# Routed experts in an attention stream: up products with the experts' weights stationary, activations kept by inner unit

## The chip, the cores and the metric

The kernel runs on one core of a Trainium2 chip. The metric is the time of one execution in microseconds, lower being better. Times are compared as medians over runs on the same chip; the reading of the engines comes from one profiled execution.

## The reference

Two transformer layers run over 32 sequences of 256 tokens of width 128, all in float32. Each layer is adaptively normalised attention with 16 heads of 8, followed by 16 routed experts of inner width 64, of which each token takes two. Layer 1 has a shared expert of width 256 besides. Cut to the routed experts, which are what the change touches:

```python
# layer 0
gu = jnp.einsum('th,ehf->tef', x, gate_up_proj) + gate_up_proj_bias
gate, up = gu[..., ::2], gu[..., 1::2]
gate = jnp.minimum(gate, LIMIT)
up = jnp.clip(up, -LIMIT, LIMIT)                       # LIMIT = 7
act = (up + 1.0) * gate * jax.nn.sigmoid(gate * ALPHA) # ALPHA = 1.702
out = jnp.einsum('tei,eih,te->th', act, down_proj, scores)
out = out + jnp.einsum('te,eh->th', scores, down_proj_bias)
# layer 1, for each expert
h = jax.nn.silu(x @ wg) * (x @ wu)
acc = acc + cw[:, None] * (h @ wd)
```

`scores` and `cw` are zero except for the two chosen experts, so only those two have to be computed.

## The kernel before

**The stream.** The attention of both layers is cut into 32 chunks of 512 tokens, and each chunk into 16 steps, 512 steps in all. In every step TensorE (PE) computes scores twice (line 1767, `s`): once for the maxima of the unit 12 steps ahead, which VectorE (DVE) reduces at line 1150 (`mpad`), and once for the exponentials, which ScalarE (ACT) takes at line 1174 (`ex`). Eight products with the values follow (line 1186, `pv`). The banks that hold the scores for the maxima are two while experts run, and three otherwise. PE's scores of the next step therefore wait for DVE's reductions of this one. All other work of the layer (projections, transposes, norms, routing) hangs on one of the 16 places of a chunk, by tables of functions. The program order of every engine is written by this one loop over steps: nothing reorders it later.

**The experts.** Tokens are sent to DRAM rows sorted by expert (`hs`), one 128-token tile for one expert. A group is 8 chunks (the last has 6) and fills 80 tiles (64), in batches of four. Groups 0 and 1 are of layer 0, groups 2 and 3 of layer 1. Groups 0 to 2 run inside the stream, one batch in three steps, 60 batches in all; group 3 runs behind the stream, one batch a step, and is called quick. For a batch that begins at step s0, the loop plans in the stream:

- `load_bias` at s0-1 (layer 0 only): four DMAs, each sending one expert's 128 biases from the DRAM table `bgt` to all 128 partitions (`bg`, line 1325); `load` at s0-5: four DMAs of token rows (`hl`, line 1315).
- `turn` at s0: four transposes of the tokens (line 1358), copied by ACT (`keep_turned`, line 1364).
- `up` at s0+1: four products, tokens stationary, the expert's gate and up weights (128 columns) moving, read from `weights` at an offset in a PE register (line 1371, `gu`). The result has tokens on partitions.
- `act_1` at s0+2, `act_1b` at the end of s0+2 (layer 0, tanh on ACT) and `act_2` at s0+4: the activation, on DVE, lines 1388 to 1408. In layer 1 `act_1` does all of it.
- `turn_act` at s0+4: four transposes back to inner units on partitions (line 1414, `aT`), copied by ACT at s0+5 (`keep_act`, line 1418).
- `down` at s0+5 (line 1425, `y`), `weigh` at s0+6 on DVE (line 1436, `yw`), `put` at s0+6 (line 1443), the DMA back to DRAM.

The functions of a step are queued in three lists. `early` comes ahead of the step's reductions on DVE, `behind_` after them, and `late` is PE's work at the end of the step. Small products for routing and the shared expert (`jobs`) run at the end of steps divisible by three; batches begin at steps that leave a remainder of one, so a job falls on s0+2 when there is one. The reductions of a step stand on DVE behind everything in `early`. SyncE (SP) issues nearly all DMAs in program order, eight completion semaphores in turn, so that a DMA waits for the one eight before it.

Of the kernel before, what the change touches and what calls it, by code (L numbers as in the profile page):

```python
# [19 lines left out]
E, FI, FS = 16, 64, 256  # L20
EPS = 1e-5
P = 128
# [3 lines left out]
NT = CT // P  # L26
# [14 lines left out]
NPAIR = E // 2  # L41
ALPHA, LIMIT = 1.702, 7.0
# [34 lines left out]
V_BQ, V_BK, V_SQ, V_SK, V_KONE, V_QONE, V_BO, V_BG, V_BU, V_SG = 0, 2, 4, 6, 8, 9, 10, 11, 19, 27  # L77
# [4 lines left out]
def two_layers(  # L82
# [50 lines left out]
    dram = ctx.enter_context(tc.tile_pool(name="dram", bufs=1, space=bass.MemoryType.DRAM))  # L133
# [1 line left out]
    hs = [dram.tile([g.rows, HR], F32, tag=f"hs{g.k}", name=f"hs{g.k}") for g in groups]  # L135
    ys = [dram.tile([P * g.tiles, D], F32, tag=f"ys{g.k}", name=f"ys{g.k}") for g in groups]
    rows = [dram.tile([B, 7 * D], F32, tag=f"rows{l}", name=f"rows{l}") for l in range(2)]
    bgt = dram.tile([E, 2, FI], F32, tag="bgt", name="bgt")
    ctx.enter_context(
        tc.manual_schedule(engines={et.PE, et.Activation, et.DVE, et.Pool, et.SP})  # L140
    )
# [32 lines left out]
    vec = loaded("vec", vecs, [P, NVEC], nc.scalar)  # L174
# [165 lines left out]
    def constants_3():  # L340

        nc.gpsimd.iota(part, [[0, 1]], base=0, channel_multiplier=1, allow_small_or_imprecise_dtypes=True)
        nc.gpsimd.memset(ones, 1.0)
        nc.gpsimd.iota(iota_e, [[0, NT], [1, E]], base=0, channel_multiplier=0, allow_small_or_imprecise_dtypes=True)
        nc.gpsimd.memset(empty, 0.0)
        nc.gpsimd.iota(tile0, [[P, TILES]], base=0, channel_multiplier=0, allow_small_or_imprecise_dtypes=True)
        nc.gpsimd.memset(aT[FI : FI + 1], 2.0)
        nc.vector.tensor_scalar(below, pos[:, :P], part, None, ALU.is_gt)
        for s_, t in ebase.items():
            nc.vector.tensor_scalar(t, iota_e, float(s_), None, ALU.mult)  # L350
        nc.vector.tensor_scalar(upto, pos[:E, :E], part[:E], None, ALU.is_ge)
        nc.vector.tensor_copy(wr1g[:, E : E + 1], vec[:, V_SG : V_SG + 1])
        for g in groups:
            nc.sync.dma_start(hs[g.k][E * g.stride :, :], empty)
# [137 lines left out]
    def expert_biases():  # L492


        def pe(p):
            nc.tensor.transpose(p[: 2 * NPAIR, :P], vec[:, V_BG : V_BG + 2 * NPAIR], ident)

        def others(p):
            b_ = once.tile([P, NT, FI], F32, tag="s", name="bts")[: 2 * NPAIR]
            b_ = b_.rearrange("p q n -> p (q n)")[:, :P]  # L500
            nc.scalar.copy(b_, p[: 2 * NPAIR, :P])
            for n in range(2):
                for a_ in range(2):
                    nc.sync.dma_start(
                        bgt.rearrange("(q a) n i -> a n q i", a=2)[a_, n],
                        b_[n * NPAIR : (n + 1) * NPAIR, a_ * FI : (a_ + 1) * FI],
                    )

        return ("bt", pe, others)
# [724 lines left out]
    def table_jobs(g):  # L1234
# [71 lines left out]
            (f"look{k}", look_up, looked_up),  # L1306
        ]

    hl, es, bgs, xTs, gus, acs, yps, yws, pst, mids = {}, {}, {}, {}, {}, {}, {}, {}, {}, {}

    def load(g, b):
# [4 lines left out]
            if b == 0 and q == 0:  # L1316
                behind(ins, scattered[k])

    def load_bias(g, b):
        k = g.k  # L1320
        if g.l == 0:
            bgs[k, b] = once.tile([P, NT, 2 * FI], F32, tag="bg", name=f"bg{k}_{b}")
            flat = bgt.rearrange("e n i -> (e n i)").rearrange("(o f) -> o f", o=1)
            for q, v in enumerate(held(tables[k][:, 0, b * NT : (b + 1) * NT], et.SP, (E - 1) * P)):
                nc.sync.dma_start(
                    bgs[k, b][:, q, :], flat[:, bass.ds(v, P)].to_broadcast([P, P])
                )

# [4 lines left out]
    def bank_of(g, b, usual, n, name):  # L1333
        if begins_at[g.k, b] < NU - 1:
            return bank(usual, name)
        if n == 2 and b % 2 == 0:
            return bank("b", name)
        return end_bank(3 if n == 1 and b % 2 else n, name)
# [27 lines left out]
    def up(g, b):  # L1366
        k = g.k
        p = bank_of(g, b, "a", 2, f"gu{k}_{b}")
        gus[k, b] = p.rearrange("p (q n) -> p q n", q=NT)
        for q in range(NT):  # L1370
            nc.tensor.matmul(  # L1371
                gus[k, b][:, q, :],
                xTs[k, b][:, q, :],
                weights[g.l][0][:, bass.ds(es[k, b][q], P)],
                start=True,
                stop=True,
            )

    def act_1(g, b):
        k = g.k  # L1380
        gate, upv = gus[k, b][:, :, :FI], gus[k, b][:, :, FI:]
        s = once.tile([P, NT, FI], F32, tag="s", name=f"s{k}_{b}")
        a_ = once.tile([P, NT, FI], F32, tag="a", name=f"a{k}_{b}")
        acs[k, b] = a_
        if g.l == 0:
            g1 = once.tile([P, NT, FI], F32, tag="g1", name=f"g1{k}_{b}")
            bg = bgs[k, b]
            nc.vector.tensor_tensor(g1, gate, bg[:, :, :FI], ALU.add)
            nc.vector.tensor_tensor(a_, upv, bg[:, :, FI:], ALU.add)
            nc.vector.tensor_scalar(g1, g1, LIMIT, None, ALU.min)  # L1390
            nc.vector.tensor_scalar(a_, a_, LIMIT, -LIMIT, ALU.min, ALU.max)
            mids[k, b] = s, g1
        else:
            nc.scalar.activation(s, gate, AF.Tanh, scale=0.5)
            nc.vector.scalar_tensor_tensor(a_, s, 1.0, gate, ALU.add, ALU.mult)
            nc.vector.tensor_tensor(a_, upv, a_, ALU.mult)

    def act_1b(g, b):
        if g.l == 0:
            s, g1 = mids[g.k, b]  # L1400
            nc.scalar.activation(s, g1, AF.Tanh, scale=ALPHA / 2)

    def act_2(g, b):
        if g.l == 0:
            k = g.k
            s, g1 = mids[k, b]
            nc.vector.scalar_tensor_tensor(g1, s, 1.0, g1, ALU.add, ALU.mult)
            nc.vector.scalar_tensor_tensor(acs[k, b], acs[k, b], 1.0, g1, ALU.add, ALU.mult)

    def turn_act(g, b):  # L1410
        k = g.k
# [182 lines left out]
    for g in groups:  # L1594

        base = max(16 * (g.end + 1) + 11, free_from)
        if g is groups[-1]:

            base = max(base, NU - 1)
        else:  # L1600
            base += (1 - base) % 3
        starts[g.k] = base

        quick = g is groups[-1]
        products, rest = {}, {}
        for b in range(g.batches):
            s0 = base + b * (1 if quick else 3)
            begins_at[g.k, b] = s0
            back, end_ = (2, 4) if quick else (4, 6)

            plan(s0 - (1 if b else 2), early, load_bias, g, b)
            plan(s0 - ((3 if quick else 5) if b else 2), early, load, g, b)
            plan(s0 + 2, behind_, act_1b, g, b)
            plan(s0 + end_, behind_, put, g, b)
            for f, at in ((turn, 0), (up, 1), (down, back + 1), (turn_act, back)):
                products.setdefault(s0 + at, {})[f] = b
            for f, at in ((weigh, end_), (keep_act, back + 1), (act_2, back), (act_1, 2), (keep_turned, 1)):
                if quick:
                    rest.setdefault(s0 + at, {})[f] = b
                else:  # L1620
                    plan(s0 + at, early, f, g, b)
        for at, what in rest.items():

            for f in (keep_turned, act_1, act_2, weigh, keep_act):
                if f in what:
                    plan(at, early, f, g, what[f])
        for at, what in products.items():

            for f in (turn, up, down, turn_act) if quick else (turn_act, down, turn, up):
                if f in what:  # L1630
                    plan(at, late, f, g, what[f])
        free_from = s0 + 3
        done[g.k] = s0 + end_
        if g.l == 0:
            assert done[g.k] < 16 * (g.first + NCHUNK - 3) + 13, (g.k, done[g.k])
# [274 lines left out]
```

## Time and profile before

| | |
|---|---|
| median of 3 runs | 1776.97 us (1776.05 to 1781.66) |
| the profiled execution | 1783.62 us |
| its span | 1781.9 us, 1.7 us less than its time |
| granted TensorE clock, mean | 0.972 |
| PE / DVE / ACT / POOL busy | 94% / 75% / 55% / 40% of the span |

The sections of the profile's page are: busy time by engine, the span in 40 slices, DMA queues, the chain that ended last, groups of instructions by line with busy time and mean duration, and DMA issues. In every row of groups the part behind the last bar is the idle time ahead of it and what ended that. Records of matmuls overlap: a matmul lasts some 270 ns even where the next one starts 110 ns later. Spacing from start to start is what PE's time is made of, and for that one reads the timeline.

### The profile page before, as it was taken

The page shows a single profiled execution, that of the slowest core. Times are in us where ns is not written, and L with a number is a line of the kernel's source. Part 1 is how long each engine was busy: PE and PEld are TensorE (multiplying, and loading weights), DVE is VectorE, ACT ScalarE, POOL GpSimd, SP SyncE. Part 2 cuts the span into 40 slices and gives each one's busy share as a digit, 9 for nine tenths or more (in the row PEclk, how much of TensorE's full clock was granted, in tenths as well). Part 3 has the DMA queues.
Part 4 walks back from the last instruction along what each step waited for, and adds up shares of the span by engine and source line. Part 5 has one row for each costly group of instructions (what it writes and reads, how often), then busy time and mean ns, then how long its engine had stood idle before and what let it go on. Part 6 is the DMA issues. An engine that isn't in the chain of part 4 may idle for free.

```text
span 1781.9 us, 45990 instructions
## 1 busy us (share of the span) xinstructions
PE 1679.8 (94%) x17025; PEld 1040.6 (58%) x17025; DVE 1343.5 (75%) x3811; ACT 971.6 (55%) x1602; POOL 717.7 (40%) x697
## 2 busy tenths in 40 slices
PE   7999999999999999999999999999999999998897
PEld 3555555555656665555666665555656666546754
DVE  6677777777768877786888887888776767755677
ACT  2566666666546666664546555655665455543333
POOL 2013333332212335664334344555543343553374
PEclk9999999999999999998999999999999999978899
DMA  2132112112445432223444544122332331234532
GB/s 58 41 77 67 47 49 63 49 45 63 105 108 126 106 91 57 56 59 79 111 112 114 95 96 103 45 50 63 99 85 74 81 96 51 69 110 107 139 93 81
DMA packets 211137, 143.38 MB, mean 80 GB/s; under 512 B 33410, under 2 KB 195618, under 8 KB 210914
## 3 DMA queue, kind: packets, MB, share of 16 engines
q1 hardware_dynamic: 187954, 108.65, 24.5%
q0 software_dynamic: 22528, 31.61, 7.1%
q8 instruction: 138, 2.26, 0.5%
q14 instruction: 85, 0.69, 0.1%
q10 hardware_dynamic: 432, 0.16, 0.0%
HBM read 76.91 MB, written 44.62 MB: 68 GB/s over the span
## 4 chain that ended last, share of the span: by engine, by line
PE 42%; DVE 13%; ACT 3%; issue 2%; DMA 2%; POOL 1%; SPq 0%; DVEq 0%; POOLq 0%; ACTq 0%
PE s L1767 14%; PE pv L1186 6%; DVE mpad L1150 3%; PE y L1425 3%; PE gu L1371 3%; PE su L1550 1%; PE aT L1414 1%; PE so L1567 1%; PE t L1358 1%; PE lp L643 1%; PE sg L1539 1%; PE vp L950 1%; PE tp L971 1%; ACT ex L1174 1%; DVE yw L1436 1%
## 5 line engine op out<-in xcount | busy, mean ns | idle before, releaser
L1174 ACT ACTIVATE ex<-s 128x1024 f32<-128x1024 f32 x512 | 523.4, 1022 | 473.9 <-PE s L1767 471.1
L1150 DVE TENSOR_REDUCE mpad<-s 128x2 f32<-128x512 f32 x1018 | 656.9, 688 | 159.1 <-PE s L1767 156.3
L1767 PE MATMUL s<-ka,qa 32*128 32x256 f32 x4096 | 639.4, 414 | 20.5 <-DVE mpad L1150 18.5
L1767 PE MATMUL s<-qa,ka 32*128 32x256 f32 x4096 | 591.2, 406 | 6.6 <-DMA qa<-mc 3.6
L1767 PEld LDWEIGHTS s<-ka,qa 32*128 32x128 f32 x4096 | 376.5, 189 | 198.4 <-DVE mpad L1150 75.1
L1767 PEld LDWEIGHTS s<-qa,ka 32*128 32x128 f32 x4096 | 357.6, 187 | 31.2 <-ACT ex L1174 15.6
L855 POOL DMA_INDIRECT yt<-ys,gslot x220 | 253.5, 1152 | 206.3 <-DVE gslot L832 68.6
L1186 PE MATMUL pv<-ex,vaug 128*32 128x256 f32 x4096 | 332.9, 397 | 3.2 <-ACT cu L964 1.3
L786 POOL DMA_INDIRECT hs<-hrow,slot x240 | 248.0, 1033 | 199.5 <-DVE yt L874 84.1
L1186 PEld LDWEIGHTS pv<-ex,vaug 128*32 128x32 f32 x4096 | 81.2, 109 | 170.1 <-issue 153.4
L769 POOL TENSOR_TENSOR oh<-oh,at 128x128 f32<-128x128 f32 x30 | 14.7, 490 | 257.3 <-DVE at L767 257.3
L534 POOL TENSOR_TENSOR rstd_a<-ve_a,mhalf 128x4 f32<-128x4 f32 x32 | 33.7, 1054 | 174.7 <-DVE ve_a L527 172.1
L1425 PE MATMUL y<-wdd,aT 65*128 (+1 forms) x608 | 89.5, 291 | 0.7 <-ACT aT L1418 0.7
L1425 PEld LDWEIGHTS y<-wdd,aT 65*128 65x128 f32 (+1 forms) x608 | 77.2, 198 | 17.6 <-issue 12.3
L1364 ACT COPY xT<-t 128x512 f32<-128x512 f32 x76 | 44.4, 584 | 78.7 <-PE t L1358 46.4
L1371 PE MATMUL gu<-wgu,xT 128*128 x608 | 86.1, 288 | 0.0
L1371 PEld LDWEIGHTS gu<-wgu,xT 128*128 128x128 f32 x608 | 79.8, 205 | 0.1
L1418 ACT COPY aT<-aT 64x512 f32<-64x512 f32 x76 | 43.9, 577 | 52.2 <-PE aT L1414 51.1
L614 POOL TENSOR_TENSOR xn_b<-xn_b,bc 128x512 f32<-128x512 f32 x32 | 41.0, 1281 | 73.1 <-ACT xn_b L551 73.1
L607 POOL TENSOR_TENSOR wog<-wo,bc 128x256 f32<-128x256 f32 x32 | 31.7, 989 | 82.7 <-DMA bc<-rows 46.2
L551 ACT ACTIVATE xn_a<-x,off_a,rstd_a 128x128 f32<-128x128 f32 x128 | 56.2, 491 | 12.6 <-DVE off_a L540 12.6
L1436 DVE TENSOR_TENSOR yw<-y,hl 128x512 f32<-128x512 f32 x76 | 52.0, 684 | 9.0 <-PE y L1425 8.7
(226 smaller groups left out, 2227.7 us busy)
## 6 DMA issues: line engine op xcount, KB each, us to landing
hl<-hs SPq DMA_DIRECT2D x304, 64.5 KB
ys<-yw SPq DMA_DIRECT2D x76, 256.0 KB
bc<-rows SPq DMA_DIRECT2D x32, 384.0 KB
bg<-bgt SPq DMA_DIRECT2D x160, 64.0 KB
ka<-kc SPq DMA_DIRECT2D x128, 64.0 KB
qa<-qc SPq DMA_DIRECT2D x64, 128.0 KB
hs<-empty SPq DMA_DIRECT2D x68, 64.5 KB
x<-in_x_dram SPq DMA_DIRECT2D x16, 256.0 KB
```

Source lines behind the costliest of these rows:

```text
L551: nc.scalar.activation(xns[C, ab][:, t, :], xs[c][:, t, :], AF.Identity, bias=off[:, t : t + 1], scale=rstd[:, t : t + 1],)
L786: ins = nc.gpsimd.indirect_dma_start(out=hs[g.k], out_offset=bass.IndirectOffsetOnAxis(ap=slots[C][:, k, t : t + 1], axis=0), in_=hrows[C] ...
L855: ins = nc.gpsimd.indirect_dma_start(out=(yt2s if apart_ else yts)[C][:, t, :], out_offset=None, in_=ys[g.k], in_offset=bass.IndirectOffse ...
L1150: nc.vector.tensor_reduce(to_, sc_, AX.X, ALU.max, negate=True)
L1174: nc.scalar.activation(ex, sc, AF.Exp)
L1186: nc.tensor.matmul(pvs[C, i][j * W : (j + 1) * W, s, :], vaug[C % 2][:, i * NQ + n, s * ST + j, a, :], ex[:, j % 2, n * S : (n + 1) * S], ...
L1364: nc.scalar.copy(xTs[k, b], pst[k, b])
L1371: nc.tensor.matmul(gus[k, b][:, q, :], xTs[k, b][:, q, :], weights[g.l][0][:, bass.ds(es[k, b][q], P)], start=True, stop=True,)
L1418: nc.scalar.copy(aT[:FI], pst["a", g.k, b][:FI])
L1425: nc.tensor.matmul(yps[k, b][:, q, :], aT[:kk, q, :], weights[g.l][1][:kk, bass.ds(es[k, b][q], P)], start=True, stop=True,)
L1436: nc.vector.tensor_tensor(yws[k, b], yps[k, b], hl[k, b][:, :, H_W : H_W + 1].to_broadcast([P, NT, D]), ALU.mult)
L1767: nc.tensor.matmul(out_, lhs, rhs, start=True, stop=True)
```

## The change

For the 60 batches in the stream the up product is turned round. The weights of each tile's expert are copied by DMA within SBUF to a fixed tile `wt`, and stand still in 64 columns at a time; the tokens move. Gate and up values come out with inner units on partitions, two tiles side by side (partitions 0 to 63 and 64 to 127). That is the layout the down product needs, so `turn_act` and `keep_act` are not planned for these batches; the last DVE operation writes `aT` itself, in two halves. Biases of layer 0 become one number per partition, fetched as 64 pairs per tile from a table laid out in pairs; bias and limit become one operation. `act_2` moves from s0+4 to s0+3, `down` from s0+5 to s0+4, `weigh` and `put` from s0+6 to s0+5. Group 3 keeps the old way (`by_token`).

```diff
-    def load_bias(g, b):
+    def load_weights(g, b):
...
+        if by_token(g, b):
+            return
+        wts[k, b] = once.tile([P, NT, 2 * FI], F32, tag="wt", name=f"wt{k}_{b}")
         if g.l == 0:
-            bgs[k, b] = once.tile([P, NT, 2 * FI], F32, tag="bg", name=f"bg{k}_{b}")
...
+            bgs[k, b] = small.tile([P, NT // 2, 2], F32, tag="bg", name=f"bg{k}_{b}")
+        flat = bgt.rearrange("e i n -> (e i n)")
+        for q, v in enumerate(held(tables[k][:, 0, b * NT : (b + 1) * NT], et.SP, (E - 1) * P)):
+            h = q % 2
+            nc.sync.dma_start(wts[k, b][:, q, :], weights[g.l][0][:, bass.ds(v, P)])
+            if g.l == 0:
                 nc.sync.dma_start(
-                    bgs[k, b][:, q, :], flat[:, bass.ds(v, P)].to_broadcast([P, P])
+                    bgs[k, b][h * FI : (h + 1) * FI, q // 2, :],
+                    flat[bass.ds(v, P)].rearrange("(i n) -> i n", n=2),
                 )
...
     def up(g, b):
+        if not by_token(g, b):
+            gus[k, b] = p.rearrange("p (n q t) -> p n q t", n=2, t=P)
+            for n in range(2):
+                for q in range(NT):
+                    h = q % 2
+                    nc.tensor.matmul(
+                        gus[k, b][h * FI : (h + 1) * FI, n, q // 2, :],
+                        wts[k, b][:, q, n * FI : (n + 1) * FI],
+                        xTs[k, b][:, q, :],
...
+    def halves():
+        for h in range(2):
+            yield (
+                slice(h * FI, (h + 1) * FI),
+                aT[:FI].rearrange("p (q h) t -> p h q t", h=2)[:, h],
+            )
...
-            nc.vector.tensor_tensor(g1, gate, bg[:, :, :FI], ALU.add)
-            nc.vector.tensor_tensor(a_, upv, bg[:, :, FI:], ALU.add)
-            nc.vector.tensor_scalar(g1, g1, LIMIT, None, ALU.min)
-            nc.vector.tensor_scalar(a_, a_, LIMIT, -LIMIT, ALU.min, ALU.max)
+            for q in range(NT // 2):
+                nc.vector.tensor_scalar(
+                    g1[:, q], gate[:, q], bg[:, q, 0:1], LIMIT, ALU.add, ALU.min
+                )
+                nc.vector.tensor_scalar(
+                    a_[:, q], upv[:, q], bg[:, q, 1:2], LIMIT + 1.0, ALU.add, ALU.min
+                )
...
             nc.vector.scalar_tensor_tensor(a_, s, 1.0, gate, ALU.add, ALU.mult)
-            nc.vector.tensor_tensor(a_, upv, a_, ALU.mult)
+            for r, to in halves():
+                nc.vector.tensor_tensor(to, upv[r], a_[r], ALU.mult)
...
             nc.vector.scalar_tensor_tensor(g1, s, 1.0, g1, ALU.add, ALU.mult)
-            nc.vector.scalar_tensor_tensor(acs[k, b], acs[k, b], 1.0, g1, ALU.add, ALU.mult)
+            for r, to in halves():
+                nc.vector.scalar_tensor_tensor(to, a_[r], 1.0 - LIMIT, g1[r], ALU.max, ALU.mult)
...
-            back, end_ = (2, 4) if quick else (4, 6)
+            back, end_ = (2, 4) if quick else (3, 5)
-            plan(s0 - (1 if b else 2), early, load_bias, g, b)
+            plan(s0 - (1 if b else 2), early, load_weights, g, b)
...
-            for f in (turn, up, down, turn_act) if quick else (turn_act, down, turn, up):
+            for f in (turn, up, down, turn_act) if quick else (down, turn, up):
```

More of the change, by code (lines that the diff above doesn't have):

```diff
@@ L137, in two_layers @@
     rows = [dram.tile([B, 7 * D], F32, tag=f"rows{l}", name=f"rows{l}") for l in range(2)]
-    bgt = dram.tile([E, 2, FI], F32, tag="bgt", name="bgt")
+    bgt = dram.tile([E, FI, 2], F32, tag="bgt", name="bgt")
     ctx.enter_context(
@@ L347, in constants_3 @@
         nc.gpsimd.memset(aT[FI : FI + 1], 2.0)
+        nc.vector.tensor_scalar(
+            vec[:, V_BU : V_BU + NPAIR], vec[:, V_BU : V_BU + NPAIR], 1.0, None, ALU.add
+        )
         nc.vector.tensor_scalar(below, pos[:, :P], part, None, ALU.is_gt)
@@ L504, in others @@
                     nc.sync.dma_start(
-                        bgt.rearrange("(q a) n i -> a n q i", a=2)[a_, n],
+                        bgt.rearrange("(q a) i n -> a n q i", a=2)[a_, n],
                         b_[n * NPAIR : (n + 1) * NPAIR, a_ * FI : (a_ + 1) * FI],
@@ L1307, in table_jobs @@
         ]
+    wts = {}
     hl, es, bgs, xTs, gus, acs, yps, yws, pst, mids = {}, {}, {}, {}, {}, {}, {}, {}, {}, {}
@@ L1317, in load, with by_token @@
                 behind(ins, scattered[k])
-    def load_bias(g, b):
+    def load_weights(g, b):
         k = g.k
+        if by_token(g, b):
+            return
+        wts[k, b] = once.tile([P, NT, 2 * FI], F32, tag="wt", name=f"wt{k}_{b}")
         if g.l == 0:
-            bgs[k, b] = once.tile([P, NT, 2 * FI], F32, tag="bg", name=f"bg{k}_{b}")
-            flat = bgt.rearrange("e n i -> (e n i)").rearrange("(o f) -> o f", o=1)
-            for q, v in enumerate(held(tables[k][:, 0, b * NT : (b + 1) * NT], et.SP, (E - 1) * P)):
+            bgs[k, b] = small.tile([P, NT // 2, 2], F32, tag="bg", name=f"bg{k}_{b}")
[4 more added lines that the diff above has]
+            if g.l == 0:
                 nc.sync.dma_start(
-                    bgs[k, b][:, q, :], flat[:, bass.ds(v, P)].to_broadcast([P, P])
-                )
+                    bgs[k, b][h * FI : (h + 1) * FI, q // 2, :],
+                    flat[bass.ds(v, P)].rearrange("(i n) -> i n", n=2),
+                )
+    def by_token(g, b):
+        return begins_at[g.k, b] >= NU - 1
     homes = [0]
@@ L1368, in up @@
         p = bank_of(g, b, "a", 2, f"gu{k}_{b}")
+        if not by_token(g, b):
[7 more added lines that the diff above has]
+                        xTs[k, b][:, q, :],
+                        start=True,
+                        stop=True,
+                    )
+            return
         gus[k, b] = p.rearrange("p (q n) -> p q n", q=NT)
@@ L1377, in up @@
             )
+    def halves():
[4 more added lines that the diff above has]
+            )
     def act_1(g, b):
         k = g.k
-        gate, upv = gus[k, b][:, :, :FI], gus[k, b][:, :, FI:]
-        s = once.tile([P, NT, FI], F32, tag="s", name=f"s{k}_{b}")
-        a_ = once.tile([P, NT, FI], F32, tag="a", name=f"a{k}_{b}")
+        s, a_ = (
+            once.tile([P, NT, FI], F32, tag=tag, name=f"{tag}{k}_{b}") for tag in "sa"
+        )
         acs[k, b] = a_
+        if by_token(g, b):
+            gate, upv = gus[k, b][:, :, :FI], gus[k, b][:, :, FI:]
+            nc.scalar.activation(s, gate, AF.Tanh, scale=0.5)
+            nc.vector.scalar_tensor_tensor(a_, s, 1.0, gate, ALU.add, ALU.mult)
+            nc.vector.tensor_tensor(a_, upv, a_, ALU.mult)
+            return
+        gate, upv = gus[k, b][:, 0], gus[k, b][:, 1]
+        s, a_ = (v.rearrange("p (q n) i -> p q (n i)", q=NT // 2) for v in (s, a_))
         if g.l == 0:
-            g1 = once.tile([P, NT, FI], F32, tag="g1", name=f"g1{k}_{b}")
+            g1 = once.tile([P, NT // 2, P], F32, tag="g1", name=f"g1{k}_{b}")
             bg = bgs[k, b]
[L1388 to L1392, printed above, removed]
+            for q in range(NT // 2):
+                nc.vector.tensor_scalar(
+                    g1[:, q], gate[:, q], bg[:, q, 0:1], LIMIT, ALU.add, ALU.min
+                )
+                nc.vector.tensor_scalar(
+                    a_[:, q], upv[:, q], bg[:, q, 1:2], LIMIT + 1.0, ALU.add, ALU.min
+                )
+            mids[k, b] = s, g1, a_
         else:
@@ L1395, in act_1 @@
             nc.vector.scalar_tensor_tensor(a_, s, 1.0, gate, ALU.add, ALU.mult)
-            nc.vector.tensor_tensor(a_, upv, a_, ALU.mult)
+            for r, to in halves():
+                nc.vector.tensor_tensor(to, upv[r], a_[r], ALU.mult)
     def act_1b(g, b):
         if g.l == 0:
-            s, g1 = mids[g.k, b]
+            s, g1, _ = mids[g.k, b]
             nc.scalar.activation(s, g1, AF.Tanh, scale=ALPHA / 2)
@@ L1404, in act_2 @@
         if g.l == 0:
-            k = g.k
-            s, g1 = mids[k, b]
+            s, g1, a_ = mids[g.k, b]
             nc.vector.scalar_tensor_tensor(g1, s, 1.0, g1, ALU.add, ALU.mult)
-            nc.vector.scalar_tensor_tensor(acs[k, b], acs[k, b], 1.0, g1, ALU.add, ALU.mult)
+            for r, to in halves():
+                nc.vector.scalar_tensor_tensor(to, a_[r], 1.0 - LIMIT, g1[r], ALU.max, ALU.mult)
     def turn_act(g, b):
@@ L1614, in two_layers @@
             plan(s0 + end_, behind_, put, g, b)
-            for f, at in ((turn, 0), (up, 1), (down, back + 1), (turn_act, back)):
+            for f, at in ((turn, 0), (up, 1), (down, back + 1)) + (((turn_act, back),) if quick else ()):
                 products.setdefault(s0 + at, {})[f] = b
-            for f, at in ((weigh, end_), (keep_act, back + 1), (act_2, back), (act_1, 2), (keep_turned, 1)):
+            for f, at in ((weigh, end_), (act_2, back), (act_1, 2), (keep_turned, 1)) + (
+                ((keep_act, back + 1),) if quick else ()
+            ):
                 if quick:
```

## The prediction

> **What bounds the kernel now.** I read the page first, then the windows for the stages, then the timeline of one batch. The page and its chain:
>
> ```profile
> PE 1679.8 (94%) x17025; PEld 1040.6 (58%) x17025; DVE 1343.5 (75%) x3811; ACT 971.6 (55%) x1602; POOL 717.7 (40%) x697
> ...
> PE 42%; DVE 13%; ACT 3%; issue 2%; DMA 2%; POOL 1%; SPq 0%; DVEq 0%; POOLq 0%; ACTq 0%
> ```
>
> PE leads and DVE is second. The stages are cut at the exponentials of steps 157, 217, 283, 343, 412 and 472; the three that carry experts (60 steps, 20 batches each) are the ones from 444.00, 828.00 and 1261.50. Columns: length, then busy PE, PEld, DVE, ACT, POOL.
>
> ```profile
> 444.00:655.10 211.10, 198.94 (x2168) 133.77 (x2167) 163.98 (x475) 122.81 (x205) 52.91 (x54) 0.98 0.45 108
> 655.10:828.00 172.90, 166.94 (x1888) 97.21 (x1884) 139.82 (x399) 106.13 (x165) 103.09 (x93) 0.99 0.26 64
> 828.00:1064.70 236.70, 222.84 (x2248) 146.09 (x2244) 187.69 (x544) 125.96 (x212) 91.69 (x83) 0.97 0.46 104
> ...
> 1261.50:1493.30 231.80, 223.19 (x2275) 145.59 (x2267) 169.74 (x477) 127.27 (x216) 93.79 (x85) 0.99 0.32 83
> ```
>
> A step takes 3.52, 3.95 and 3.86 us with experts and 172.9/66 = 2.62 us between them. DVE is busy 73 to 79% there, so PE's spacing is the first thing to count. One batch in layer 0:
>
> ```profile
> 606.93 0.44 PEld L1414 LDWEIGHTS aT<-ident,a 128*64 128x64 f32 x4
> 607.04 0.60 PE L1414 MATMUL aT<-ident,a 128*64 128x128 f32 x4
> 607.37 0.97 PEld L1371 LDWEIGHTS gu<-wgu,xT 128*128 128x128 f32 x8
> 607.48 1.06 PE L1371 MATMUL gu<-wgu,xT 128*128 x8
> ...
> 608.58 0.42 DVE L1388 TENSOR_TENSOR g<-gu,bg 128x256 f32<-128x256 f32 x1 [0.95 <-PE gu L1371]
> 608.92 0.41 DVE L1389 TENSOR_TENSOR a<-gu,bg 128x256 f32<-128x256 f32 x1
> 609.25 0.28 DVE L1390 TENSOR_SCALAR g<-g 128x256 f32<-128x256 f32 x1
> 609.36 1.85 SPq L1325 DMA_DIRECT2D bg<-bgt  x4
> 609.45 0.29 DVE L1391 TENSOR_SCALAR a<-a 128x256 f32<-128x256 f32 x1
> ...
> 609.65 1.28 DVE L1150 TENSOR_REDUCE mpad<-s 128x2 f32<-128x512 f32 x2
> ```
>
> The reader should see three things. The transposes hold PE from 607.04 to 607.48, 0.44 us, and up takes 8 records 0.11 apart. The activation stands on DVE ahead of the reductions for which PE's next scores wait. The four biases cost SP 1.85 us.
>
> From the starts of all matmul records I also sorted the steps of a batch by kind (s0, s0+1, s0+2). PE's own spacing, waits left out, is 2.7, 3.6 and 3.2 us in the first stage (4.1 and 4.2 for s0+2 in the others, where a job falls on it). The steps really last 2.8, 4.2, 3.4; 3.1, 4.1, 4.3; and 3.2, 3.8, 4.7. So about 90% of an expert step is PE spacing, and a step without expert or job has 2.2.
>
> **The change part by part.** *Transposes.* Four a batch go, each 0.109 us start to start: 0.436 us, times 60 is 26.2 us off PE. The copy behind them (577 ns) leaves ACT, 60 x 0.48 = 29 us by spacing; ACT is at 55% and I count nothing.
>
> *Up.* Eight products become sixteen records of 64 stationary columns, 128 moving. Whether the two halves run together decides their price. The nearest rows are quarters of 32 columns:
>
> ```profile
> 453.07 0.64 PE L1186 MATMUL pv<-ex,vaug 128*32 128x256 f32 x8
> 453.52 1.04 PE L902 MATMUL kp<-hT_a,w 128*32 128x512 f32 x8
> 454.50 0.49 PE L1767 MATMUL s<-ka,qa 32*128 32x256 f32 x2
> ```
>
> Eight kp records of 592 ns, 512 moving columns each, occupy PE for 0.98 us, where one after the other they would need 3.4 (0.427 each at the 107 ns that 128 columns take); four run at once. For two halves, sixteen records are then 8 x 0.109 to 0.12 = 0.87 to 0.96 us against 8 x 0.111 = 0.89 now: -1 to +4 us over 60 batches, I take 0.
>
> *A switch of shape.* Down (128 columns) now stands directly ahead of up (64). Between shapes PE loses time in some rows: pv to a 128-wide transpose takes 0.310 where the 256 columns need 0.213, a transpose to the scores 0.203 instead of 0.109, each some 0.096 us. But the present aT (64 columns) to gu takes 0.108, nothing lost. So 0 to 0.096 x 60 = 0 to 5.8 us, less 1.1 for the 11 batches whose down had a step to itself among the wide work. I take +2, between the two rows. [...]
>
> PE together: -26.2 + 0 + 2 = -24 us.
>
> *DVE.* In layer 0, lines 1388 to 1391 (0.34 + 0.33 + 0.20 + 0.20 = 1.07 us by spacing) become four operations of 128x128 with a pointer scalar, each between 0.20 (16x128 `wshift`, L1280) and 0.26 (128x128 `so`, L1579): 0.80 to 1.04. act_2 gets a third operation, 0.34 each: 1.02 for 0.68. In layer 1 one more at 0.34. Busy time: 40 x (0.07 to 0.31) + 20 x 0.34 = 10 to 19 us more; it costs only where it delays the reductions. That is a matter of place. Step s0+2 loses down from PE (0.99 us) and gains weigh (0.60) on DVE ahead of act_1. If up's 0.9 us hides weigh, since down ends before up starts, the reductions end 0.1 + 1.04 + 1.20 = 2.35 us after the scores begin, against PE's 2.2: 0.15 lost. If it hides nothing, 2.95: 0.75 lost. In s0 act_2 takes the place of weigh, 1.02 for 0.60: 0 to 0.3 lost, as that step has 0.15 of slack. First stage: 20 x (0.15 to 1.05) = 3 to 21 us. In the other stages a job keeps s0+2 at 3.1 us of PE; only places without other wide work are short, and in layer 1 act_1 also waits for tanh (0.39): 0 to 0.3 x 40 = 0 to 12. Together 3 to 33 us. I take 9, near the lower end, as weigh's input is there a whole up product earlier.
>
> *Where stalls go.* Down waited for aT's copy on ACT; now for act_2, planned a step ahead of it. What is late next is the reductions, just priced.
>
> *SP and the DMAs.* Layer 0 issues eight DMAs a batch for four, layer 1 four for none, each 0.333 us and some 0.5 with its register work: +2 us per batch on SP, where issues and table loads took 126 of the 211 us of the first stage. load_weights stays at s0-1, in the queue between load of the next batch and put of an earlier one; it now waits for the previous up, as `wt` is one tile. Queued behind it are the sends of q, k and the maxima (`qa<-mc`), on which PE's scores depend, and put. The trace's semaphore records (no view prints them) give landings after issue: hl 2.3 us in the median (4.7 at nine in ten), ka from SBUF 2.1, but bg 4.8 and each bg some 1.5 after the last. From the end of one up to the start of the next there is one batch less up: 10.5 - 0.9 = 9.6 us. The last weights are issued as the seventh of eight, 3.5 us in, and land 2.1 to 4.7 later: 5.6 to 8.2 us. Hidden, with 1.4 to 4 us in hand; no charge. If the cover is gone, every us late costs 40 us over layer 0. The bias pieces of 8 bytes have no row; bounds are 0 and bg's 1.5 us apiece, and at the upper bound the four take no more of the queue than the four bg do now. [...]
>
> Sum: -24 + 9 = -15 us against the profiled execution's own 1783.6 (span 1781.9): 1768.6. The median of the runs shown is 6.6 us lower, so 1762. Group 3 and everything behind the stream (168.9 us) stay as they are.
>
> **The rivals.** (1) DVE takes it all back: weigh, act_1 and the longer act_2 stand ahead of the reductions in s0+2 and s0, and nothing hides them. At the upper 33 us the sum is +9: 1786. For it: DVE is already at 79% in the second stage, and the wait list has scores waiting for mpad. Against: in s0+1 DVE gets nothing new and catches up. It decides from the point where weigh starts after up has ended; slower begins where the loss passes 24 us, 0.4 us a batch.
> (2) The weights land late, PE waits at gu: 1 us per batch of layer 0 is +40, 1802. For it: eight issues behind one another and waits in SP's order. Against: the 1.4 us in hand even at the slow landing.
> (3) The halves do not run together: 16 x 0.109 = 1.74, +0.85 x 60 = 51, 1813. Against: kp and pv. That would be the change not doing what it says.
> (4) More: the slow bg transfers no longer hold the queue. In the expert stages PE lost 3.4 and 0.9 us to `qa<-mc` and 1.9 and 3.2 to the first `hl`; without these 9 us it is 1753.
>
> **How the numbers follow.** Forecast 0.50, with its own range 1752 to 1773; rival 1 0.20, rival 2 0.08, rival 3 0.05, rival 4 0.17. A difference of 0.3%, about 5 us, is what can be told from no change. Faster: 0.47 of the forecast, all of rival 4 and 0.02 of rival 1, 0.66. Same: 0.03 + 0.07 = 0.10. Slower: 0.11 of rival 1, rivals 2 and 3: 0.24. The range 1746 to 1788 leaves out rivals 2 and 3 and thin tails, under 2 in 10.
>
> **What would show it.** aT gone but for group 3; sixteen gu records of 64 columns in pairs some 0.11 apart, the group about 0.9 us; y to gu between 0.11 and 0.21. Step s0+1 longer by some 0.55, s0+2 shorter by 0.5 to 0.9. ACT busy some 30 us less, DVE 10 to 19 more, PE's scores waiting longer for mpad. Wrong: gu waiting for a DMA `wt`, gu records one by one, or s0+2 no shorter although down has left it.

## The result, and the profile after

The changed kernel is slower: 1809.99 us in the median (1800.72 to 1815.26), the kernel before 1779.11; ratio 1.016 with an interval of 1.013 to 1.020. Its profiled execution took 1810.9 us (span 1809.1), 27.3 more than that of before (1783.6). The same sections of its page, engines and chain:

```profile
PE 1683.3 (93%) x17265; PEld 1019.8 (56%) x17265; DVE 1375.0 (76%) x3872; ACT 939.0 (52%) x1542; POOL 716.7 (40%) x697
...
PE 62%; DVE 20%; ACT 4%; SPq 4%; issue 4%; POOL 3%; DMA 2%; DVEq 0%; ACTq 0%; POOLq 0%
```

ACT is 32.6 us less busy (30 were foreseen) and DVE 31.5 more (10 to 19). PE is no less busy, although its transposes are gone. In the chain SP's queue now has 4%; it had 0%. The windows of the same stages, cut at the same exponentials (length, busy PE, PEld, DVE, ACT, POOL, then the granted clock):

```profile
444.70:685.40 240.70, 212.95 (x2252) 135.41 (x2248) 173.14 (x496) 112.38 (x186) 52.59 (x54) 0.95 0.36 96
685.40:858.30 172.90, 167.07 (x1884) 96.97 (x1880) 138.80 (x398) 105.50 (x163) 102.68 (x92) 0.99 0.26 63
858.30:1110.40 252.10, 226.72 (x2332) 142.10 (x2335) 198.89 (x564) 116.10 (x194) 91.12 (x83) 0.95 0.40 98
1307.30:1530.20 222.90, 214.39 (x2358) 136.07 (x2351) 181.39 (x498) 116.67 (x197) 92.26 (x83) 1.00 0.42 109
```

The first stage of layer 0 is 29.6 us longer and the second 15.2; layer 1's is 8.8 shorter, and the stage without experts is the same. The last 39 steps take 2.4 us more, and what follows them 12.2 less. With a microsecond of scatter this is the 27.3. One batch of the first stage, answering to the batch shown of before:

```profile
538.06 1.09 PE L1392 MATMUL gu<-xT,wt 128*64 128x128 f32 x16
538.17 0.69 DVE L1487 TENSOR_TENSOR yw<-y,hl 128x512 f32<-128x512 f32 x1 [0.27 <-PE y L1476]
...
540.25 1.29 DVE L1154 TENSOR_REDUCE mpad<-s 128x2 f32<-128x512 f32 x2
...
542.26 0.39 DVE L1457 SCALAR_TENSOR_TENSOR g<-s,g 128x256 f32<-128x256 f32 x1
...
542.69 0.85 DVE L1459 SCALAR_TENSOR_TENSOR aT<-a,g 64x256 f32<-64x256 f32 x2
543.57 0.69 DVE L1017 TENSOR_TENSOR x<-y,x 128x512 f32<-128x512 f32 x1
...
544.18 1.28 DVE L1154 TENSOR_REDUCE mpad<-s 128x2 f32<-128x512 f32 x2
```

The product does what was meant: sixteen records take 1.09 us where eight took 1.06, so two halves run at once, and `weigh` lies beside them. Two steps on (s0 of the next batch) act_2 holds DVE from 542.26 to 543.54, the residual's addition (line 1017) comes behind it, and the reductions begin only at 544.18. But the stage's largest losses are elsewhere. SP 25 us earlier, with the maxima that it sends:

```profile
507.00 0.34 ACT L1029 COPY mc<-mT 16x256 f32<-16x256 f32 x1
...
512.41 0.53 SPq L1335 DMA_DIRECT2D wt<-wgu  x1
513.17 0.49 SPq L1337 DMA_DIRECT2D bg<-bgt  x1
...
517.68 1.35 SPq L1034 DMA_DIRECT2D qa<-mc  x2
...
519.61 0.79 PE L1820 MATMUL s<-qa,ka 32*128 32x256 f32 x2 [3.94 <-DMA qa<-mc]
```

The maxima lie ready at 507.3. SP first issues a `put`, four `hl` and two smaller loads, then the eight DMAs of a batch, one every 0.65 us (0.49 to 0.53 for the issue, the rest register work), and sends the maxima at 517.68. PE has stood for 3.9 us when they arrive. The list of PE's waits for DMAs in this stage (us in all, times, longest), the first line before, the others now:

```profile
PE s L1767 <- DMA qa<-mc: 3.1, 1, 3.1
...
PE s L1820 <- DMA qa<-mc: 9.9, 3, 3.9
PE s L1820 <- DMA qa<-qc: 4.5, 2, 2.5
PE gu L1392 <- DMA wt<-wgu: 3.2, 5, 0.9
```

In this stage SP's instructions took 126 us of 211 before and take 192 of 241 now (a sum from the trace; SP's own waits not counted). No wait of SP in it is for a landing of an earlier DMA, so the eight completion semaphores do not hold it. And PE's stall is not all of its price, as short windows from 518 on show (the third number from the end is the granted clock):

```profile
518.00:520.00 2.00, 0.39 (x4) 0.42 (x8) 0.00 (x0) 0.00 (x0) 0.00 (x0) 0.74 0.06 9
520.00:522.00 2.00, 2.00 (x16) 1.06 (x16) 1.11 (x2) 0.22 (x1) 0.00 (x0) 0.50 0.63 178
...
528.00:530.00 2.00, 2.00 (x24) 1.22 (x24) 1.57 (x8) 0.04 (x1) 0.00 (x0) 0.70 0.11 33
530.00:532.00 2.00, 1.20 (x14) 0.49 (x10) 1.93 (x6) 1.76 (x3) 0.00 (x0) 1.00 0.14 33
```

From 519.0 the clock is half for some 10 us, in which PE loses up to another 5.1 us. Over the whole stage, by its mean clock, that comes to at most (1 - 0.95) x 240.7 = 12 us, where before it was (1 - 0.98) x 211 = 4.

### The profile page after: what moved, and what is told of

It reads as the page before. It is cut to its first block, busy times and chain, and to the rows that moved or that the text cites. A ratio compares the mean times of both kernels' runs of the same rounds, so it can differ in the third digit from the quotient of the medians.

```text
span 1809.1 us, 46670 instructions
## 1 busy us (share of the span) xinstructions
PE 1683.3 (93%) x17265; PEld 1019.8 (56%) x17265; DVE 1375.0 (76%) x3872; ACT 939.0 (52%) x1542; POOL 716.7 (40%) x697
## 4 chain that ended last, share of the span: by engine, by line
PE 62%; DVE 20%; ACT 4%; SPq 4%; issue 4%; POOL 3%; DMA 2%; DVEq 0%; ACTq 0%; POOLq 0%
PE s L1820 26%; PE pv L1190 10%; DVE mpad L1154 6%; PE y L1476 4%; PE gu L1392 3%; PE lp L647 2%; PE vp L954 2%; PE so L1618 1%; PE t L1375 1%; PE tp L975 1%; ACT ex L1178 1%; PE kp L906 1%; PE su L1601 1%; ACT xn_b L555 1%; POOL hrow L620 1%
## 5 line engine op out<-in xcount | busy, mean ns | idle before, releaser
L1820 PE MATMUL s<-ka,qa 32*128 32x256 f32 x4096 | 656.8, 416 | 38.0 <-DVE mpad L1154 29.8
L1820 PEld LDWEIGHTS s<-ka,qa 32*128 32x128 f32 x4096 | 386.3, 190 | 230.7 <-DVE mpad L1154 105.7
L1392 PE MATMUL gu<-xT,wt 128*64 128x128 f32 x960 | 72.7, 292 | 3.2 <-DMA wt<-wgu 3.2
L1392 PEld LDWEIGHTS gu<-xT,wt 128*64 128x64 f32 x960 | 55.9, 144 | 12.5 <-DMA wt<-wgu 4.7
L1375 PE MATMUL t<-ident,hl 128*128 128x128 f32 x304 | 50.3, 286 | 8.2 <-DMA hl<-hs 5.4
## 6 DMA issues: line engine op xcount, KB each, us to landing
hl<-hs SPq DMA_DIRECT2D x304, 64.5 KB
hs<-empty SPq DMA_DIRECT2D x68, 64.5 KB
```

The source lines that it names most:

```text
L1375: nc.tensor.transpose(p[:, q, :], hl[k, b][:, q, :D], ident)
L1392: nc.tensor.matmul(gus[k, b][h * FI : (h + 1) * FI, n, q // 2, :], wts[k, b][:, q, n * FI : (n + 1) * FI], xTs[k, b][:, q, :], start=True, ...
L1820: nc.tensor.matmul(out_, lhs, rhs, start=True, stop=True)
```

## The experiments

Theory A: SP runs out of issue time. Theory B: act_2 and act_1 on DVE ahead of the reductions. Theory C: the weights land late. Where several runs ask one question they stand together. Seven runs fell on two chips where the kernel before took 1974 and 1997 us: the first each with the places of before, with biases copied by ACT, with biases issued by ACT and with the later combine, and the three made from the kernel before. There only ratios, and stages of the same chip, are compared.

Stage lengths in us, between the exponentials of the same steps, and the clock in the two stages of layer 0, on the faster chips:

| kernel | first | second | layer 1 | clock | ratio to before |
|---|---|---|---|---|---|
| before | 211.0 | 236.8 | 231.7 | 0.98, 0.97 | 1 |
| after | 240.6 | 252.0 | 222.9 | 0.95, 0.95 | 1.016 (1.013 to 1.020) |
| change in layer 1 alone | 209.9 | 235.6 | 223.2 | 0.98, 0.98 | 0.989 (0.985 to 0.992) |
| no bias DMAs | 207.4 | 249.2 | 222.9 | 1.00, 0.95 | 0.997 (0.994 to 0.999) |
| no weight DMAs | 207.0 | 249.1 | 223.1 | 1.00, 0.94 | 0.997 (0.993 to 1.000) |
| neither | 213.8 | 246.8 | 222.9 | 0.96, 0.95 | 0.995 (0.992 to 0.998) |
| four one-element DMAs for the biases | 234.3 | 252.2 | 222.9 | 0.93, 0.95 | 1.013 (1.011 to 1.016) |
| biases issued by ACT | 219.2 | 251.8 | 223.0 | 0.97, 0.93 | 1.014 (1.012 to 1.017) |
| two buffers for weights | 232.9 | 248.5 | 222.9 | 0.94, 0.96 | 1.015 (1.008 to 1.022) |
| places of before | 234.2 | 242.1 | 222.9 | 0.95, 0.96 | 1.002 (0.998 to 1.005) |
| places of before, biases copied by ACT | 198.1 | 228.9 | 223.2 | 1.00, 1.00 | 0.974 (0.968 to 0.981) |

**Which layer loses.** The change for layer 1 alone; layer 0 gets the code and places of before:

```diff
-        return begins_at[g.k, b] >= NU - 1
+        return begins_at[g.k, b] >= NU - 1 or g.l not in (1,)
...
-            back, end_ = (2, 4) if quick else (3, 5)
+            by_turn = quick or g.l not in (1,)
+            back, end_ = (2, 4) if quick else (4, 6) if by_turn else (3, 5)
```

> The change is made in layer 1 alone (groups 0 and 1 keep the transposed activation, the products with the tokens' stationary and the broadcast biases). Both theories put the loss in layer 0, so both expect the stages of layer 0 as before (211 and 237 us) and the stage of layer 1 as after (223 for 232): some 9 us under the kernel before, 1768 to 1772. If layer 1 gives nothing by itself (its gain in the trace of after came from something that layer 0 shifted), the time is that of before, 1779.

1758.3 us. The stages came as expected, but the total is 10 to 14 us below the 1768 to 1772 expected, by what follows the stream. Layer 1 by itself is a gain, and the whole loss is layer 0's.

**DMAs left out.** The fetches of biases, of weights, and of both, in layer 0; the operations read four fixed columns, and the products four fixed experts' weights, in their place:

```diff
-            bgs[k, b] = small.tile([P, NT // 2, 2], F32, tag="bg", name=f"bg{k}_{b}")
+            bgs[k, b] = vec[:, V_BG : V_BG + NT].rearrange("p (q n) -> p q n", n=2)
-            if g.l == 0:
-                nc.sync.dma_start(
...
-        wts[k, b] = once.tile([P, NT, 2 * FI], F32, tag="wt", name=f"wt{k}_{b}")
+        if g.l:
+            wts[k, b] = once.tile([P, NT, 2 * FI], F32, tag="wt", name=f"wt{k}_{b}")
+        else:
+            wts[k, b] = weights[0][0][:, : NT * P].rearrange("p (q n) -> p q n", q=NT)
...
-            nc.sync.dma_start(wts[k, b][:, q, :], weights[g.l][0][:, bass.ds(v, P)])
+            if g.l:
+                nc.sync.dma_start(wts[k, b][:, q, :], weights[g.l][0][:, bass.ds(v, P)])
```

> The changed kernel, but layer 0 fetches no biases: the operations read four fixed columns of the constants in their place (the biases are left out of the result). Theory A (SP is full: eight issues of 0.50 to 0.52 us, 0.65 to 0.78 apart, delay the sends of maxima and q for which the scores wait): four issues less are 2.7 us of SP per batch, the first expert stage falls from 241 to 205 to 215 us, the second by a few, the time to some 1770 to 1780. Theory B (the operations on DVE ahead of the reductions): DVE's work is the same, so less than 5 us is gained, 1805 or more. Theory C (the weights land late): the weights are then issued one behind the other, the last after 2.2 instead of 4.8 us, so C expects a gain too, but of the waits at gu alone, some 5 us.

> The changed kernel, but layer 0 fetches no weights: its up products read four fixed experts' columns (so the result is another in layer 0); the four biases are still fetched. Theory A: four issues less, 3 us of SP per batch, much the same as without the biases, 1770 to 1780. Theory B: 1805 or more. Theory C: all waits at gu for a DMA go, 5 us, 1805.

> The changed kernel with neither biases nor weights fetched in layer 0 (both left out as in the two runs before, and the four register loads on SP with them): all the work on PE, DVE and ACT stays. Theory A: SP has 6 us per batch less than in the changed kernel and 3 less than in the kernel before, the first expert stage takes some 200 to 205 us and the time is 1755 to 1768. Theory B: what DVE costs stays, the first stage keeps at least half of its 30 us more, the second its 15, time 1790 or more.

1773.9, 1773.5 and 1766.4 us. Either four less take 33 us off the first stage, and it does not matter which four: C falls, since without biases the weights are still fetched. In the first stage without biases, by the same list of PE's waits, those for `qa<-mc` shrink from 9.9 us to 0.2 and those for `qa<-qc` (4.5) and `wt` (3.2) go. Its clock:

```profile
444.40:651.80 207.40, 197.91 (x2252) 127.57 (x2248) 172.53 (x496) 112.17 (x186) 52.69 (x54) 1.00 0.41 110
```

The same number of matmul records is 15 us less busy in the first stage than in the changed kernel, at most 12 of them by the clock, which never falls there. The second stage keeps 12 of its 15 us with four DMAs less and 10 with none of the eight: A does not explain it. Taking away all eight was expected to gain more than four; in the first stage it did not (213.8, with two spells of half clock), so A's own price list was too simple as well.

**Place on DVE.** The changed kernel with layer 0's steps where they were before, on two chips:

```diff
-            back, end_ = (2, 4) if quick else (3, 5)
+            back, end_ = (2, 4) if quick else (4, 6) if g.l == 0 else (3, 5)
```

> The changed kernel with all its products and DMAs, but in layer 0 act_2 (s0+4), down (s0+5) and weigh and put (s0+6) stand where they stood in the kernel before. Theory A (SP) and theory B (DVE: three act_2 operations ahead of the reductions of step s0) have shares: B is 0.6 us a batch in the first expert stage and 1.2 in the second (step s0's loss in the median, which stayed when the DMAs were gone), A is what the missing four issues gave in the first stage, 33 us. So the second stage falls from 252 to 225 to 232, the first from 241 to 228 to 238 since SP still issues eight, and the time is 1775 to 1785. If B is wrong (the loss sits in the products or in the operations themselves and not in their place), both stages stay, 1805 or more. If the place were all, the first stage would fall below 205 too, 1745.

> The run with the places back once more, on a chip where the kernel before takes some 1780 us if there is one (it took 1974 us where it was first tried, with the tail behind the last exponential at 212 us instead of 157): the stages are to be compared with those of the changed kernel. A and B with shares: second expert stage 225 to 238 for 252, first 225 to 238 for 241, ratio 0.995 to 1.003.

Ratios 1.008 (1.003 to 1.012) and, on a faster chip, 1.002. The second stage falls by 10 us, to 242.1 where 225 to 238 were expected, and the first by 6. By kind of step (medians, from the starts of the scores' matmul records) step s0 lasts 3.5 and 3.9 us in the changed kernel's two stages, 3.4 and 3.9 without the bias DMAs, but 2.9 and 3.1 with the places back, against some 2.7 of PE's own spacing. So s0 pays 0.6 us a batch in the first stage and 0.8 in the second, whatever SP does. The run moves act_2, down, weigh and `put` together; that it is the reductions behind act_2 shows in PE's waits of the second stage, for the kernel before, the changed one, that without bias DMAs, and that with the places back:

```profile
PE s L1767 <- DVE mpad L1150: 1.9, 4, 0.8
...
PE s L1820 <- DVE mpad L1154: 12.6, 10, 2.3
...
PE s L1815 <- DVE mpad L1154: 12.9, 11, 2.4
...
PE s L1820 <- DVE mpad L1154: 2.9, 5, 1.0
```

Not all of it comes back: the other two steps of a batch take 0.2 to 0.3 us more, and in the first stage PE has a new wait:

```profile
PE gu L1392 <- DMA wt<-wgu: 10.0, 11, 2.2
PE s L1820 <- DMA qa<-mc: 9.3, 3, 4.1
```

With DVE out of the way, up is earlier at the door of the weights.

**Both mended.** The places back, and the biases copied by ACT from a table that stays in SBUF:

```diff
...
-                nc.sync.dma_start(
-                    bgs[k, b][h * FI : (h + 1) * FI, q // 2, :],
-                    flat[bass.ds(v, P)].rearrange("(i n) -> i n", n=2),
-                )
...
+            for q, v in enumerate(held(tables[k][:, 2, b * NT : (b + 1) * NT], et.Activation, 2 * (E - 1))):
+                h = slice(q % 2 * FI, (q % 2 + 1) * FI)
+                nc.scalar.copy(bgs[k, b][h, q // 2, :], bres[0][h, bass.ds(v, 2)])
...
```

> As the run with the places back, and layer 0's biases are copied by ACT (four copies of 64x2 with a register's offset) from a table that stays in SBUF, in place of four DMAs: SP has four issues a batch as before. A and B together: first stage 198 to 207 us, second 225 to 232, the time 1740 to 1752. If ACT's four copies and register loads delay the exponentials (ACT is busy 53%), some 0.5 to 1 us a batch comes back: 1760 to 1785.

> The run with the places back and the biases copied by ACT once more, for the same reason. In the first trial the first stage took 208 us and the second 251, where layer 0 left as before took 214 and 260 on that chip. Here 198 to 207 and 222 to 230, time 1740 to 1752, ratio 0.980 to 0.985, if A and B are the whole loss; the share of layer 1 and its tail is 0.9885 by itself.

Ratios 0.990 (0.986 to 0.994) and 0.974 (0.968 to 0.981); on the faster chip 1738.4 us, the best of all versions, below both kernels and below the 1740 to 1752 expected. The two stages of layer 0:

```profile
443.50:641.60 198.10, 190.66 (x2252) 123.36 (x2253) 172.19 (x494) 126.77 (x261) 51.89 (x53) 1.00 0.43 114
814.80:1043.80 229.00, 212.51 (x2332) 133.28 (x2336) 195.38 (x563) 130.32 (x270) 91.64 (x83) 1.00 0.42 106
```

PE's clock is whole in both. A copy of 64x2 takes 188 ns on ACT, four are 0.75 us a batch. For layer 0's two stages the four corners are 492.6 (after), 456.6 (four DMAs less), 476.3 (places) and 427.0 us (both): 16 + 36 = 52 would be the sum of the single effects, together they are 66. SP and DVE each hide a part of the other's loss.

**SP in the kernel before.** The four weight DMAs added, to a tile that nothing reads; and the reverse, the biases of a group's first batch kept for the others:

```diff
+                nc.sync.dma_start(wt[:, q, :], weights[0][0][:, bass.ds(v, P)])
...
-        if g.l == 0:
+        if g.l == 0 and b:
+            bgs[k, b] = bgs[k, 0]
+        elif g.l == 0:
```

> The kernel before, with the four weight pieces of the changed kernel also fetched per batch of layer 0, to a tile that nothing reads. Theory A alone: the same work on PE, DVE and ACT as before, and SP at eight issues a batch: the first stage grows by 15 to 33 us, the second by 0 to 5, time 1795 to 1815. Theory B alone: 1779. It is less than in the changed kernel where the biases' issue is cheaper here (0.33 us for 0.50), and nothing waits for the weights.

> The kernel before, but the biases of a group's first batch are fetched once and serve its other batches (so layer 0's biases are wrong for these): SP has four issues a batch less than before, all other work is the same. If SP's issues and the slow broadcasts cost something before too, the first stage falls from 211 by 5 to 10 us and the second from 237 by 0 to 6, ratio 0.991 to 0.996; what the version with biases by ACT gains beyond that is the change's own. If they cost nothing at four a batch, 211 and 237 stay, ratio 1.000.

Ratios 1.013 (1.009 to 1.017) and 0.991 (0.988 to 0.995), both on slower chips. With four more the first stage is 232.9 us for 213.5 in the kernel with layer 0 as before on that chip; with four less 208.1 for 214.0 and the second 252.8 for 260.1. So four more DMAs on SP, with nothing else changed, cost the first stage 19 us, where the change cost it 30. And the issues cost something at four a batch already, so, as far as ratios from two chips can be set off, 0.9 of the 2.6% of the best version would be had without the change, if the biases came without DMAs.

**Waiting or issuing.** In the changed kernel SP waits 68 us in all for an earlier up product to free `wt`; by windows 5.6 of them lie in the first stage, 17.7 in the second and 44.8 in layer 1's, which loses nothing. Two buffers:

```diff
-        wts[k, b] = once.tile([P, NT, 2 * FI], F32, tag="wt", name=f"wt{k}_{b}")
+        wts[k, b] = work.tile([P, NT, 2 * FI], F32, tag="wt", name=f"wt{k}_{b}")
```

> The changed kernel, with two buffers for the fetched weights in place of one, so that their issue on SP no longer stands waiting for the previous up product (68 us of SP in 27 waits in the trace of after) with the sends behind it. Theory A1 (the mere number of issues fills SP; the waiting takes time in which SP would stand anyway): little changes, ratio to the kernel before 1.010 to 1.017. Theory A2 (the waiting blocks the queue): a good part of what four issues less gave comes back, ratio 0.995 to 1.003.

1.015 (1.008 to 1.022), A1: the number of issues, and not the waiting among them, fills SP. With 5.6 us of that wait in the first stage there was little for A2 to win.

**Issues or transfers.** Four one-element DMAs in the places of the biases'; the biases' DMAs issued by ACT with its own registers, on two chips; and the kernel without bias DMAs on the chip of the former:

```diff
+                nc.sync.dma_start(scrap[0][:1, q : q + 1], vec[:1, q : q + 1])
...
-                nc.sync.dma_start(
...
+        for q, v in enumerate(held(tables[k][:, 0, b * NT : (b + 1) * NT], et.Activation, (E - 1) * P)):
...
+            nc.scalar.dma_start(
+                bgs[k, b][h * FI : (h + 1) * FI, q // 2, :],
```

> The changed kernel without its bias DMAs (biases left out as in the run without them), but with four DMAs of one element each in their places on SP: they move nothing to speak of and nothing reads them. Theory A (SP's issue time): if a tiny one costs SP 0.33 to 0.5 us as the others do, the first stage is 225 to 241 us, the ratio 1.005 to 1.017. Theory D (the pieces that the biases move): the first stage stays at 207, ratio 0.997.

> The changed kernel with its places, and the four bias DMAs of a batch issued by ACT in place of SP: the same eight transfers with the same pieces, but SP issues four. Theory A (SP's issue time is what runs out): the first stage falls from 241 to 207 to 222 us (ACT now spends some 2 us a batch on issues, which can delay exponentials), the ratio to the kernel before is 0.995 to 1.005. Theory D (the transfers themselves crowd the DMA engines or the queue, whoever issues them): the first stage stays at 233 to 241, ratio 1.010 to 1.017.

> The changed kernel with its bias DMAs issued by ACT, once more: in its first trial the kernel before took 1997 us, and the first stage 235 us for 214 in the kernel before there, with waits for the exponentials and not for the sends. Theory A with ACT's own price: PE's waits for the sends of q and the maxima go, and waits for ACT's exponentials come, 41 us of issues on ACT in the first stage; first stage 215 to 235, ratio 1.000 to 1.017. Theory D: the waits for the sends stay.

> The run without bias DMAs, for one profile beside the two above: its first stage is what the four tiny DMAs are compared with, 207 us where the kernel before takes 1780 in all.

The tiny ones cost as much as the biases: 234.3 us in the first stage where the kernel without them has 209.0 beside it, ratio 1.013. One takes SP 0.588 us:

```profile
L1341 SPq DMA_DIRECT2D scrap<-vec x160: 572/588/722, 438.1 to 1091.1; - x160
```

They move four bytes each, so it is issue time and not transfer: D falls. The runs from ACT's queue (ratios 1.017 and 1.014) do not decide this by their times: the first missed what A expected of it (0.995 to 1.005) and lies, with a first stage of 235.5 us, where D had it. Their waits do: those for the sends go from PE's list of the first stage as A says, and in the second trial the stage falls to 219.2 us. But ACT now issues ahead of its exponentials, for some 0.5 us each (0.50 for the one at 529.75 in the first trial). PE waits 7.1 us for ACT's copy `cu` in the stage and once 5.2 for `ex` ahead of it, the 157 steps ahead of the stage take 8 us more and the stage without experts 6, and over the whole kernel next to nothing is won.

**The tail.** The version with layer 1 alone, its group 2's combine one step later, as before, on two chips; and another profile of the program before:

```diff
-            at, left = done[g.k] + 2, 0
+            at, left = done[g.k] + 3, 0
```

> The change in layer 1 alone (1758 us), with the combine of group 2 (find_slots and its gathers) planned from the same step as in the kernel before, one step later than the change has it. What follows the last exponential took 169 us before and 156 to 157 in every kernel with the change in layer 1. Theory T (that is the combine's earlier start): the tail goes back to 163 to 169, the time to 1765 to 1771. If the tail's gain is something else (transposes that go, the places of put), it stays at 156 and the time at 1758.

> The run with the change in layer 1 alone and the combine of group 2 from the step of the kernel before, once more. Its first trial had ratio 0.9954 where layer 1 alone has 0.9885, but on another chip. Theory T (the tail's 12 us are the earlier combine): ratio 0.994 to 0.997 and a tail of 163 to 169 us; else 0.987 to 0.990 and a tail of 156.

> The program of the kernel before, for a second profile of it: how far its stages and its tail (169 us in the first profile) vary from one execution to the next. Stages within 2 us of 396, 211, 173, 237, 197 and 232; the tail 163 to 169 if the earlier combine explains some 5 to 8 us of what every kernel with the change in layer 1 gained there, 156 if the first profile was an outlier.

Ratios 0.995 (0.993 to 0.998) and 0.995 (0.991 to 0.998), against 0.989 (0.985 to 0.992) with the earlier combine. What follows the last exponential takes 165.7 us again, as theory T said (155.8 with the earlier combine, 168.9 before). But the 39 steps ahead of it are 5 us shorter there: from step 472 to the end the profiles have 276.3 us with it, 281.0 without, 288.6 in the kernel before. So the combine, which starts a step earlier since `put` does, is 4.7 of these 12.3 us by the profiles and some 10 by the ratios, which are from different chips. How much of the rest is something else stays open: the other profile of before is from a slower chip (tail 214.6) and does not tell.

## Why the prediction was wrong, step by step

**Transposes, up and switch of shape: right in kind, a quarter too large.** The halves run in pairs. PE's own spacing, waits left out, fell by some 0.1 us a step in each of the three stages, some 18 us in all, where the sum had 24. This is an estimate: where the line between spacing and wait is drawn moves it from 16 to 28. The starts of the matmul records show where the sum was short. Up with its end, to the next scores, takes 1.024 us for 0.987, 2 us over 60 batches and not 0. From down to up PE takes 0.205 us for 0.109, the whole 0.096 that was the upper bound, so that the switch of shape costs 4 to 5 us and not 2. By the estimate step s0+1 grew (3.6 to 4.2 us of spacing) and s0+2 shrank (3.2 to 2.2) as foreseen.

**SP and the DMAs: the step that failed.** It named all of it: eight issues, 2 us a batch more on SP, the sends of q, k and maxima queued behind them. It then asked only whether the weights land before up, and charged nothing. They do land in time: PE's waits at gu for `wt` are 3.2 us in the first stage, and a piece lands 1.9 us after its issue. What had to be asked is whether SP has the time, and who stands last in its line: eight at 0.65 us are 5.2 (0.5 each were taken), and with four `hl`, two table loads, `put` and the sends SP's instructions take 192/20 = 9.6 us a batch, where a batch had 10.5. The price was not 0 but 36 us in layer 0 (492.6 less 456.6), most of it in the first stage, where a batch is shortest. In the second a batch has 11.8 us, and SP shows only once DVE is mended (242.1 to 228.9).

**DVE: the mechanism right, the size wrong.** Step s0 was given 0 to 0.3 us of loss from act_2 and has 0.6 to 0.8; three operations are 1.2 us by spacing (0.45, 0.43, 0.34), not 1.02, as half the partitions take no less time: 421 ns for 64x256 (line 1447), 424 for 128x256 (line 1428). Moving it back brings 16 us at eight DMAs and 30 at four, where 9 were charged over all. act_1 came at the upper bound, 0.259 an operation. In step s0+2, which was to lose 0.15 to 0.75, PE stood still 0.0 us in the median and 0.2 in the mean once SP was relieved (first stage, no bias DMAs).

**The rivals.** Rival 1 (DVE) is the second cause, with the longer waits for `mpad` that it named. Rival 2 looked at the right queue, but for the wrong customer: not gu, the scores wait. Rival 3 is out by the pairs. Rival 4 was right that the broadcasts held SP up: before, it waited 12.2 us for landings of `bg` ahead of other `bg` alone, and no bias DMA of the changed kernel waits so. What that cost PE isn't separated: the kernel before with its biases fetched once is 13 us shorter in layer 0, but has four issues a batch less too. (The list of waits has 3.1 and 0.5 us for `qa<-mc` and 1.9 and 3.4 for `hl`, where the rival has 3.4, 0.9, 1.9 and 3.2; the sum is 9 either way.)

**Left out altogether.** The tail, taken as fixed, gave 10 us back. And the clock: no term of the sum had it, although before's own windows at 0.97 and 0.98 show it. Of the 44.8 us lost in layer 0, (0.05 x 240.7 - 0.02 x 211.1) + (0.05 x 252.1 - 0.03 x 236.7) = 13 at most are PE at half speed. Most of it stands just behind stalls: of the 48 us of half clock in the changed kernel's two stages, 34 lie in spells that began during a wait of PE of 2.1 to 3.9 us or within 1.4 us of its end.

## What to carry to other kernels

Where one engine issues nearly all DMAs, count its issue time per period of the loop as one counts PE's, each DMA at its measured issue and register time, however few bytes it moves (0.588 us to issue one element here); when the sum comes near the period, ask which small urgent send stands last in line. Price a stall of PE with the half clock behind it, where the trace shows one (here 10.2 us of it at one of 3.9). A move that frees one engine's slot should leave the steps of the others where they had room: both faults could be mended apart from the change, and then it gains.

## What the runs showed of the hardware

- A DMA of one element from SBUF takes SP 0.588 us to issue, a 128x128 piece at a register's offset 0.516, the 64 pairs of biases 0.496, but token rows from DRAM (64.5 KB) 0.333 (medians): its time does not follow the bytes.
- In the expert stages of the kernels before and after, the granted clock falls to exactly half in spells of 3.4, 6.8 or 10.2 us (from 1587 us on also longer ones, up to 30.7); each 3.4 us at half clock costs PE up to 1.7. In the changed kernel waits of PE of 2.50 and 2.10 us (to 470.96 and 582.8) were followed by half clock within 1.0 us, but one of 2.35 us (to 932.7) was not, and the spell from 918.3 had no wait over 0.8 us just ahead of it. What sets it off is not shown.
- The program before took 1776 to 1780 us on some chips and 1974 to 1997 on others, at mean clocks of 0.97 and some 0.93, longer in every stage and most behind the stream (tail 215 for 169 us). Of ACT's waits for its exponentials 45.6 us are put down there to another core or an unknown queue. What that is stays open.
